# The scaled bias of the update as one GpSimd product, and the layer-1 bias of seven chunks in ten written by ScalarE

## The chip, the cores and the metric

The kernel runs on one core of a Trainium2 chip. The metric is device time in microseconds for one execution. A core has a matrix engine (TensorE, in the profile PE, with its weight loads shown apart as PEld), VectorE (DVE), ScalarE (ACT), GpSimd (POOL) and a queue engine SyncE (SP) that issues DMA transfers. The engines run side by side, each in the order of its own instructions, and wait for one another through semaphores. TensorE writes its results to PSUM banks; ScalarE and VectorE read them from there.

## The reference

A graph layer over 128 graphs of 64 nodes with 128 channels. Per edge (i, j) of the adjacency an MLP of three linear layers runs over the pair of node features; the messages of a node are summed, and a second MLP of the same form updates the node.

```python
def _mlp(x, w0, b0, g0, be0, w1, b1, g1, be1, w2, b2):
    h = jax.nn.relu(x @ w0 + b0)
    h = _layernorm(h, g0, be0)
    h = jax.nn.relu(h @ w1 + b1)
    h = _layernorm(h, g1, be1)
    return h @ w2 + b2

pair_feats = jnp.concatenate([f_i, f_j], axis=-1)
messages = _mlp(pair_feats, msg_w0, ...)
messages = messages * coupling_matrix[..., None]
agg = jnp.sum(messages, axis=2)
upd_in = jnp.concatenate([part_feats, agg], axis=-1)
updated = part_feats + _mlp(upd_in, upd_w0, ...)
```

`x` is 128 x 64 x 128 in f32; the coupling matrix is a sparse 0/1 matrix with self edges, about one entry in eight.

## The kernel before

**Tiling.** Two graphs make a pair (64 pairs); a graph has room for 640 edges. Four graphs make a quad with 20 tiles of 128 edges, and four tiles make a *chunk*: 160 chunks in all. Four pairs make a *block*, so a block is ten chunks and there are 16 blocks. Only real edges are computed; a dense path for graphs with more edges than fit stands at the end of the program and isn't entered here.

**The deferred norm.** The normalisation of layer 0 is not applied to the hidden values. The layer-1 weights are centred beforehand (`w1c`), so the product needs only a division by the standard deviation; as ReLU and the next norm don't mind a positive factor, the kernel multiplies the *bias* by the standard deviation instead. A tile's layer-1 result in bank `z` is therefore the product h x `w1c` plus the bias row `b1b` times each edge's standard deviation. That scaled bias comes into `z` in one of two ways. Either TensorE writes it first, by one matmul over 512 columns from a table (`b1t` and the turned standard deviations `sdT`, line 602); or ScalarE writes it into the bank beforehand, by four activations of 128 x 128 with the standard deviation as their scale (`seed`, line 593), and TensorE adds the products to it. Of ten chunks six are seeded, and the four others use line 602. The update's MLP has the same need once per block: `usdb` is the bias row `bu1b` scaled for each of the block's 512 nodes, made by four activations on ScalarE (`upd_shift`, line 773), and added by VectorE in `layer_out` (`uy`, line 238).

**The order of work.** It is written out by hand. A plan maps (step, place) to functions; a loop over steps runs, in each step n, the places "a" and "m" first (copies, small sums), then layer 1 of chunk n - 8, then "b", layer 0 of chunk n, the turning of chunk n - 1 with its statistics, "k" (marks and comparisons for a later pair), the statistics of chunk n - 8, and then the places "x" to "e". Every engine gets its instructions in that order and keeps to it. One step is therefore one chunk in each of two stages.

In a step, TensorE does: L605 (layer 1, into one of two `z` banks in turn), L535 (layer 0, into the only `hps` bank), L544 (turning h, into the only `hT` bank), L509 (marks); in some steps also L691 (sums over edges, 20 products of a pair at a time), L449/L451 (rows of a new half block), L736 and L750 (update), and L568, which turns the standard deviations of a quad (`sh`). ScalarE empties `z` into `y` (L608) and `hps` into `h` (L538), seeds (L593), and makes square roots: `m_sd` (L255) for a quad, `um_sd` (same line) for a block's update. VectorE makes statistics (L548 of layer 0, L615 of layer 1), `tp` (L484, an f16 comparison over 640 edges), `j` (L517) and more. GpSimd makes the variances from the statistics (L245 to L249, tiles `m` and `um`), the low parts `sh` (L563), the weights `w` (L678), the cast `i` of `tp` (L493), and the residual `xo` (L730).

**The step of `seed` and `upd_shift`.** The seed of chunk n is issued in step n + 6, two before its layer 1. Chunks whose number modulo 10 is 0, 1, 2, 6, 7, 9 are seeded. `upd_root0` of a block (which makes `um_sd`) and the first `usdb` copy stand in a step that is 9 modulo 10, the second copy one step later, the last two in the step after that, which is 1 modulo 10; `usdb` is read in step 2 modulo 10. In the step 9 modulo 10 stands also `residual` (`xo`). All this holds for the first 13 blocks, which follow `STEADY`; the last three have tables of their own (`LAST`).

Of the kernel before, what the change touches and what calls it, by code (L numbers as in the profile page):

```python
# [14 lines left out]
ALU = mybir.AluOpType  # L15
# [8 lines left out]
def tile_gnn(  # L24
# [40 lines left out]
    nc = tc.nc  # L65
    B, N, C = x.shape
    P = 128
# [9 lines left out]
    PB = 4  # L77
    NB = NP // PB
    CPB = NCHK // NB
# [88 lines left out]
    W = {}  # L168
# [62 lines left out]
    def bc(t, n, axis=1):  # L231

        s = [P, n, C] if axis == 1 else [P, C, n]
        return t.unsqueeze(axis).to_broadcast(s)
# [50 lines left out]
    def edge_path(es):  # L285
# [32 lines left out]
        def zbank(k):  # L318
            return ps_z[k].tile([P, CH * C], F32, name=f"z{k}")
# [4 lines left out]
        def at(n, place, fn, *args):  # L324
            plan.setdefault((n, place), []).append((fn, args))
# [382 lines left out]
        def wide(name, u):  # L708

            if name not in u.blk:  # L710
                u.blk[name] = updp.tile([P, PB, C], F32, name=name,
                                        bufs=2 if name in ("uo", "xo", "m0") else 1)
            return u.blk[name][:, u.q, :]
# [29 lines left out]
        def layer(u, *pairs):  # L743
            ps = u.bank()
            for q in range(u.n):
                s = slice(q * P, (q + 1) * P)
                for n, (src, w) in enumerate(pairs):
                    l = (u.blk["xnT"][:, (u.k0 + q) * P:(u.k0 + q + 1) * P] if src == "xn" else
                         getattr(u, src)[:, s])
                    nc.tensor.matmul(ps[:, s], lhsT=l, rhs=w, start=(n == 0),  # L750
                                     stop=(n == len(pairs) - 1))
            u.l_ps = ps[:, 0:u.n * P].rearrange("p (q c) -> p q c", q=u.n)
# [16 lines left out]
        def upd_shift(u, q0, q1):  # L769
            if q0 == 0:  # L770
                u.usdb = wide("usdb", u)
            for q in range(q0, q1):
                nc.scalar.activation(u.usdb[:, q, :], W["bu1b"], AF.Copy, scale=u.sd[:, q:q + 1])

# [54 lines left out]
        for b in reversed(range(NB)):  # L829
            o = b * CPB  # L830
            n = o + QC + SC

            if b < NB - 1:
                t = STEADY if b < NB - 3 else LAST[b - NB + 3]
                units = [(Unit(b, 0, PB, nc.gpsimd, ubank), n, t, 0, t[5] - 1)]
                if b == NB - 2:
                    units = [units[0][:3] + (-5, -4)]
            else:
                units = [(Unit(b, 2, 2, nc.vector, lambda: zbank(1), tbank), NCHK + L1 + 1, LAST[3], 1, 1),
                         (Unit(b, 0, 2, nc.gpsimd, lambda: zbank(0), hbank), NCHK + L1 - 1, LAST[2], 3, 3)]  # L840
            for u, n, t, m0_at, xo_at in units:
                at(n + m0_at, "m", bias0, u)
                at(n + xo_at, "e", residual, u)
                at(n + t[0], "a", sums_out, u)
                at(n + t[1], "x", turn, u, "ysum")
                at(n + t[2], "a", turn_out, u, "ysum")
                at(n + t[3], "x", lambda u: layer(u, ("xn", u0a), ("ysumT", W["w2u"])), u)
                at(n + t[4], "m", layer_out, u, "uh", "m0")
                at(n + t[4], "e", upd_m0, u)
                at(n + t[5], "x", turn, u, "uh")  # L850
                at(n + t[6], "a", turn_out, u, "uh")
                at(n + t[7], "a", upd_root0, u)
                if t is STEADY:
                    for k, q0, q1 in ((0, 0, 1), (1, 1, 2), (2, 2, PB)):
                        at(n + t[7] + k, "x", upd_shift, u, q0, q1)
                else:
                    at(n + t[7], "x", upd_shift, u, 0, u.n)
                at(n + t[8], "x", lambda u: layer(u, ("uhT", W["u1c"])), u)
                at(n + t[9], "m", layer_out, u, "uy", "usdb")
                at(n + t[9], "e", upd_m1, u)  # L860
                at(n + t[10], "x", turn, u, "uy")
                at(n + t[11], "a", turn_out, u, "uy")
                at(n + t[12], "a", upd_root1, u)
                at(n + t[12], "m", upd_inverse, u)
                at(n + t[13], "x", lambda u: layer(u, ("uyT", W["u2c"])), u)
                at(n + t[14], "m", finish, u)
        for p in range(NP):
            n = p * TG * 2 // CH
# [18 lines left out]
        for q in range(NQ):  # L887
            n = q * QC + QC if q else LEAD
# [10 lines left out]


        for n in range(2, NCHK - L1):
            if n % CPB in (0, 1, 2, 6, 7, 9):
                at(n + L1 - 2, "x", seed, n)


# [153 lines left out]
    with ExitStack() as es:  # L1059
        es.enter_context(tc.manual_schedule())  # L1060
        flag = edge_path(es)
# [160 lines left out]
```

## Time and profile before

| What | Value |
|---|---|
| Median of 9 runs | 575.0 us (573.81 to 577.68) |
| The profiled execution | 575.01 us |
| Its span, first to last instruction | 573.2 us |
| Granted TensorE clock | 0.989 of full speed |
| Bias matmuls L602 | 70, median 478 ns |
| Seeds L593 | 360 activations, median 371 ns |
| Copies L773 | 64 activations, median 392 ns |
| DMA | 63.23 MB moved, mean 110 GB/s |

The profile is one execution on the chip. A timeline row reads: start and duration in us, engine, line, operation, the tiles written and read, their shapes, the number of instructions merged into the row, and in brackets how long the engine was idle before it and what ended that wait. A matmul's duration includes the time that it spends in the array beside its neighbours, so its cost is read from the distance of starts. Tile names in the profile are cut: `um_sd` is the standard deviation of the update's block, `m_sd` that of a quad, `m_d` and `m_s` are intermediate sums, and `um` and `m` the variances' sums. Rows with the same line, such as L255, differ by tile.

### The profile page before, as it was taken

The numbers are of one execution on the slowest core, as the hardware profiler recorded it, in microseconds if no ns is written. First come the engines' busy times: TensorE is split into PE (matmuls) and PEld (weight loads), VectorE is DVE, ScalarE is ACT, GpSimd is POOL, SyncE is SP. The second block draws the span as 40 slices with busy tenths as digits, with TensorE's granted clock in tenths as the row PEclk, the third lists the DMA queues.
The fourth block names the chain that finished last, engine by engine and source line by source line (L and its number), as shares of the span: only waits on it lengthen the run. The fifth ranks groups of instructions, "written<-read, shape, count | busy, mean of one in ns | idle before, by whom it ended". The sixth has DMA issues, their size and how long they took to land. (4 is left out here: it accounts for less than half of the span.)

```text
span 573.2 us, 15824 instructions
## 1 busy us (share of the span) xinstructions
PE 551.8 (96%) x5339; PEld 518.5 (90%) x5339; DVE 479.5 (84%) x1944; ACT 476.3 (83%) x1149; POOL 339.6 (59%) x898
## 2 busy tenths in 40 slices
PE   8799899999999999999999999999999999989894
PEld 7587889999999999999999999999999999979883
DVE  6758788997979899797989889798989979786686
ACT  7678979898988889898988999898888989875434
POOL 3625466665657676565757666565767656545342
PEclk9889999999999999999999999999999999998999
DMA  4554646455654645644555545447454545432101
GB/s 102 124 134 110 129 113 136 91 132 112 107 149 110 132 102 143 113 112 126 125 139 107 138 106 132 107 109 153 113 137 87 127 115 108 113 93 28 39 19 42
DMA packets 90770, 63.23 MB, mean 110 GB/s; under 512 B 57398, under 2 KB 74812, under 8 KB 90684
## 3 DMA queue, kind: packets, MB, share of 16 engines
q1 hardware_dynamic: 90396, 62.03, 48.7%
q8 instruction: 44, 0.72, 0.6%
q14 instruction: 42, 0.34, 0.2%
q10 hardware_dynamic: 288, 0.13, 0.1%
HBM read 6.82 MB, written 4.19 MB: 19 GB/s over the span
## 5 line engine op out<-in xcount | busy, mean ns | idle before, releaser
L548 DVE BATCH_NORM_STATS2 st<-hT 128x6 f32<-128x128 f32 x640 | 142.0, 284 | 37.8 <-PE hT L544 36.2
L605 PE MATMUL z<-w1c,h 128*128 128x128 f32 x1280 | 172.5, 278 | 0.0
L605 PEld LDWEIGHTS z<-w1c,h 128*128 128x128 f32 x1280 | 161.5, 192 | 8.0 <-issue 5.1
L593 ACT ACTIVATE z<-b1b,m_sd 128x128 f32<-128x128 f32 x360 | 133.5, 371 | 8.7
L615 DVE BATCH_NORM_STATS2 st<-y 128x6 f32<-128x128 f32 x640 | 137.6, 277 | 2.7 <-ACT y L608 1.4
L608 ACT ACTIVATE y<-z 128x512 f32<-128x512 f32 x160 | 94.5, 591 | 26.5 <-PE z L605 24.8
L538 ACT ACTIVATE h<-hps,b0c 128x512 f32<-128x512 f32 x160 | 109.4, 684 | 2.2 <-PE hps L535 2.2
L544 PE MATMUL hT<-ident,h 128*128 128x128 f32 x640 | 97.9, 276 | 1.8 <-DVE st L548 1.6
L678 POOL TENSOR_TENSOR w<-oh,m_q 128x320 f32<-128x320 f16 x126 | 91.9, 741 | 9.9 <-PE hT L544 5.3
L535 PE MATMUL hps<-s,abl 128*128 128x512 f32 (+3 forms) x256 | 92.1, 371 | 2.0 <-ACT h L538 1.5
L544 PEld LDWEIGHTS hT<-ident,h 128*128 128x128 f32 x640 | 76.5, 141 | 12.7 <-DVE st L548 1.9
L493 POOL CAST i<-tp 128x640 fp32r<-128x640 f16 x58 | 41.6, 718 | 70.0 <-DVE tp L484 49.1
L535 PE MATMUL hps<-s,abh 128*128 128x512 f32 (+3 forms) x256 | 78.9, 327 | 0.0
L691 PE MATMUL ys<-y,w 128*64 128x128 f32 x1280 | 76.9, 275 | 0.0
L691 PEld LDWEIGHTS ys<-y,w 128*64 128x64 f32 x1280 | 69.2, 137 | 4.2 <-issue 3.6
L245 POOL TENSOR_TENSOR m_d<-st 128x20 f32<-128x20 f32 x62 | 16.3, 263 | 88.5 <-DVE st L548 76.7
L517 DVE TENSOR_TENSOR j<-mk,cmpt 128x320 fp32r<-128x320 f32 x124 | 58.7, 474 | 1.5 <-PE mk L509 1.5
L478 ACT ACTIVATE d<-slot,mid 128x640 f16<-128x640 f16 x64 | 52.7, 823 | 0.0
L535 PEld LDWEIGHTS hps<-s,abl 128*128 128x128 f32 x256 | 49.4, 193 | 3.3 <-ACT h L538 2.3
L535 PEld LDWEIGHTS hps<-s,abh 128*128 128x128 f32 x256 | 49.5, 193 | 0.0
L469 DVE TENSOR_TENSOR abl<-mu,abh 128x512 fp32r<-128x512 f32 (+1 forms) x33 | 22.3, 675 | 30.9 <-ACT abh L463 30.7
L463 ACT CAST abh<-mu 128x512 fp32r<-128x512 f32 (+1 forms) x33 | 18.9, 571 | 23.8 <-PE mu L451 23.8
(226 smaller groups left out, 1007.4 us busy)
## 6 DMA issues: line engine op xcount, KB each, us to landing
s<-i SPq DMA_DIRECT2D x124, 160.0 KB, 2.6
s<-j SPq DMA_DIRECT2D x124, 160.0 KB, 2.6
xn<-in_x_dram SPq DMA_DIRECT2D x15, 256.0 KB, 3.7
out_dram<-uo SPq DMA_DIRECT2D x15, 256.0 KB, 2.4
an<-in_adj_dram SPq DMA_DIRECT2D x16, 128.0 KB, 2.6
oh<-tp SPq DMA_TRANSPOSE x64, 3.4
xn<-in_x_dram SPq DMA_DIRECT2D x2, 128.0 KB
out_dram<-uo SPq DMA_DIRECT2D x2, 128.0 KB, 2.6
```

The costliest lines, as they stand in the source:

```text
L478: nc.scalar.activation(D[p], slot, AF.Abs, bias=blocks[b]["mid"][:, q:q + 1], scale=-1.0)
L517: nc.vector.tensor_tensor(JR[p][:, c], MK.pop((p, k))[:, 0:HC], cmpt[:, c], op=ALU.is_equal)
L535: nc.tensor.matmul(ps[:, c:c + w], lhsT=ab[:, g % 4, :], rhs=s, start=(k == 0), stop=(k == 1))
L538: nc.scalar.activation(H[n], ps, AF.Relu, bias=b0c)
L544: nc.tensor.transpose(ps[:, t, :], H[n][:, t * P:(t + 1) * P], ident)
L548: nc.vector.bn_stats(ST0[q][:, CH * c + t, :], ps[:, t, :])
L593: nc.scalar.activation(Z[n][:, t, :], W["b1b"], AF.Copy, scale=SR[q][:, k:k + 1])
L605: nc.tensor.matmul(ps[:, t, :], lhsT=h[:, t * P:(t + 1) * P], rhs=W["w1c"], start=False, stop=True, skip_group_check=True)
L608: nc.scalar.activation(Y[n], ps, AF.Relu)
L615: nc.vector.bn_stats(ST1[q][:, CH * c + t, :], Y[n][:, t, :])
L678: (nc.vector if p == NP - 2 else nc.gpsimd).tensor_tensor(WT[p][:, :, g, :], OH[p][:, :, g * N:(g + 1) * N], Q[q][:, k:k + TG].unsqueeze(2 ...
L691: nc.tensor.matmul(YS[b][g * N:(g + 1) * N, k, :], lhsT=w[:, t, g, :], rhs=y, start=(t == 0), stop=(t == TG - 1))
```

## The change

Three edits. `upd_shift` gets a branch: where it is called for all four rows of a block it issues one GpSimd product of 128 x 4 x 128, the bias row broadcast over the four node tiles times the standard deviation broadcast along the channels, in place of four ScalarE copies. For the 13 blocks that follow `STEADY` it is called so once, in place "e" of the step in which `um_sd` is made, instead of in three pieces in three steps; it thereby comes on GpSimd directly after `xo` and before the cast `i` of the next step. For the other blocks the four (or two) ScalarE copies are issued by two calls (or one) of two rows, at the same step. And the condition for seeding takes in the chunks that are 5 modulo 10 and over 10, where a seed by ScalarE replaces line 602.

```diff
         def upd_shift(u, q0, q1):
             if q0 == 0:
                 u.usdb = wide("usdb", u)
+            if q1 - q0 == PB:
+                nc.gpsimd.tensor_tensor(u.usdb, bc(W["bu1b"], PB),
+                                        u.sd.unsqueeze(2).to_broadcast([P, PB, C]), op=ALU.mult)
+                return
             for q in range(q0, q1):
                 nc.scalar.activation(u.usdb[:, q, :], W["bu1b"], AF.Copy, scale=u.sd[:, q:q + 1])
...
                 if t is STEADY:
-                    for k, q0, q1 in ((0, 0, 1), (1, 1, 2), (2, 2, PB)):
-                        at(n + t[7] + k, "x", upd_shift, u, q0, q1)
+                    at(n + t[7], "e", upd_shift, u, 0, PB)
                 else:
-                    at(n + t[7], "x", upd_shift, u, 0, u.n)
+                    for q0 in range(0, u.n, 2):
+                        at(n + t[7], "x", upd_shift, u, q0, q0 + 2)
...
         for n in range(2, NCHK - L1):
-            if n % CPB in (0, 1, 2, 6, 7, 9):
+            if n % CPB in (0, 1, 2, 6, 7, 9) or (n > CPB and n % CPB == 5):
                 at(n + L1 - 2, "x", seed, n)
```

In the code P and C are 128, PB is 4 (node tiles of a block), CPB is 10 (chunks of a block), NCHK is 160 and L1 is 8.

## The prediction

> **What bounds the kernel now.** I read the page's busy list first, then busy time by windows over three blocks, then the timeline of single stretches.
>
> ```profile
> PE 551.8 (96%) x5339; PEld 518.5 (90%) x5339; DVE 479.5 (84%) x1944; ACT 476.3 (83%) x1149; POOL 339.6 (59%) x898
> ...
> 366.61:399.46 32.85, 32.85 (x331) 31.39 (x330) 28.94 (x120) 29.32 (x72) 21.21 (x56) 1.00 0.56 122
> 399.46:432.31 32.85, 32.85 (x332) 31.40 (x330) 28.95 (x120) 29.32 (x72) 21.20 (x56) 1.00 0.54 121
> 432.31:465.16 32.85, 32.85 (x331) 31.39 (x330) 28.96 (x120) 29.33 (x72) 21.22 (x56) 1.00 0.51 118
> ```
>
> After the span the window rows give busy PE, PEld, DVE, ACT and POOL. A block (ten chunks) takes 32.85 us, the same three times over, and PE has no gap in it. DVE idles 3.9 us, ACT 3.5, POOL 11.6. A busy PE need not be a full one, but the starts of its matmuls follow each other at constant distances (0.112 us from one L605 to the next), so it is PE's own throughput that sets the block. What leaves PE is gained; what delays PE is lost. The page's chain of waits names only the last store's DVE op and is of no use.
>
> **What leaves PE.** Two stretches, one with the bias matmul L602, one without:
>
> ```profile
> 306.33 0.30 PE L509 MATMUL mk<-tp,posall 128*128 128x320 f16 x1
> 306.36 0.50 PE L602 MATMUL z<-b1t,sdT 80*128 80x512 f32 x1
> 306.70 0.38 PE L605 MATMUL z<-w1c,h 128*128 128x128 f32 x2
> ...
> 303.14 0.30 PE L509 MATMUL mk<-tp,posall 128*128 128x320 f16 x1
> 303.28 1.05 PE L750 MATMUL mu<-u1c,uhT 128*128 128x128 f32 x8
> ```
>
> From the L509 start to the next 128-column matmul it is 0.37 us with L602 between and 0.14 without: 0.23 us (0.233 in ns), not the 0.48 that the row states as L602's duration. The Trainium skill, "TensorE: Matmul & The Clock Gate", section "Back-to-back issue gap", gives columns / 2.4 + 2.5 ns for an isolated warm matmul: 216 ns at 512 columns; the trace's 233 is near it and is what I use. The new condition adds chunks 15, 25, ... 145, 14 in all: 14 x 0.233 = 3.26 us. The 306.36 instance is one of them (chunk 85).
>
> **ScalarE.** Off: four L773 per block for 13 blocks; two stand at 304.14 with 0.68 us together, so 0.29 apart, 1.17 a block. On: four L593 in 14 chunks, 1.51 us from the first to what follows (306.68 to 308.19). Net +0.34 us a block against 3.5 us idle. (The rewritten loop for the last blocks issues the same copies at the same place: nothing.) By place: the seed of chunk 85 comes in the step where two L773 stood (304.14), so that step grows by 0.92 us:
>
> ```profile
> 304.14 0.68 ACT L773 ACTIVATE usdb<-bu1b,um_sd 128x128 f32<-128x128 f32 x2
> 304.73 0.25 ACT L573 CAST sdT<-ma 80x128 fp32r<-80x128 f32 x1
> 305.61 0.60 ACT L608 ACTIVATE y<-z 128x512 f32<-128x512 f32 x1 [0.63 <-PE z L605]
> ```
>
> 0.63 of it fills the wait shown. The y after it starts about 0.2 to 0.3 us late, and so does the next h (306.10 to 306.78). PE's next L535 needs that h evacuated, since hps has one bank; it starts at 307.51, or 307.28 after the saving, so of 0.73 us some 0.2 remain. The following y and h are later still, but PE then spends 3 us on L691 and L449, and ACT catches up before L463 at 312.12 (it idled 0.59 there). The seed itself ends near 305.9; its L605 is at about 306.5. Cost: nothing, with 0.2 us of cover; every tenth beyond is paid 14 times.
>
> **GpSimd.** One 128x512 product a block. Its price: pos (L384), like it f32 with one operand broadcast along the row, takes 506 ns at 192 columns and 612 at 256, 1.66 ns a column, so 1.035 us at 512; b1t (L655), 80x512 with both operands broadcast as here, has a median of 1.034. Above stands xo (L730), 128x512 but with rows read in full: 1.274. The skill, "GPSIMD Engine Reference", section "3.1 Elementwise — side-by-side cycle accounting", has 2.6 cycles an element for two inputs, an estimate of 1.11 us plus dispatch, between the two. I take 1.035; the ends are 0.95 and 1.274.
>
> POOL has room: behind the new product in its queue are only the cast L493 and then L245, which waited 2.36 us for DVE. The j and oh transfers on SP sit behind the cast's stack copy; the cast moves 0.6 us, and its rows are read five chunks later. But the product's place decides:
>
> ```profile
> 330.33 0.31 ACT L255 ACTIVATE um_sd<-um,eps_c 128x4 f32<-128x4 f32 x1
> 330.92 0.38 DVE L484 TENSOR_SCALAR tp<-d,deg 128x640 f16<-128x640 f16 x1
> 331.37 0.72 POOL L493 CAST i<-tp 128x640 fp32r<-128x640 f16 x1 [3.52 <-DVE tp L484]
> 331.68 0.89 DVE L548 BATCH_NORM_STATS2 st<-hT 128x6 f32<-128x128 f32 x4 [0.38 <-PE hT L544]
> 332.84 0.60 PE L544 MATMUL hT<-ident,h 128*128 128x128 f32 x4
> ```
>
> It waits for um_sd (end 330.64) and, with the 0.078 us that POOL takes after ACT in the sh pair, starts at 330.72: 0.2 us before DVE's tp. The skill, "SBUF — State Buffer", section "Who interferes with whom", says that a 2-port DVE op and a GpSimd op exclude each other for the whole instruction, and "VectorE: DVE Perf Modes", section "What auto-detection actually checks", lets a 16-bit one-source SBUF op such as tp take such a mode. The trace agrees:
>
> ```profile
> 26.29 1.42 POOL L655 TENSOR_TENSOR b1t<-b1mix,tile_of 80x512 fp32r<-80x512 f32 x1
> ...
> 26.80 1.09 DVE L484 TENSOR_SCALAR tp<-d,deg 128x640 f16<-128x640 f16 x1
> ```
>
> tp took 1.09 instead of 0.37 and ended 0.18 us after the product. So here: the product ends at 331.75, tp at 331.93, the next DVE op can start 0.08 before that end, 331.85 in place of 331.68: DVE is 0.17 us late. First in line is hT at 332.84, which needs this L548 (end 332.57): 0.27 less 0.17 leaves 0.10, above the 0.056 us that PE needs after DVE in the shortest cases. Second is a chain that runs with DVE from there: L548, POOL's five sums for m, ACT m_sd, ACT sh, POOL sh, then the turn L568. sh ends at 304.00 and L568 starts 0.170 later. Where L568 really waited (75.28) it started 0.055 after sh and took 0.308 against 0.273; so slack is 0.170 - 0.055 - 0.035 = 0.08. DVE's 0.174 (in ns) exceeds it: PE loses 0.093 us. In 12 of the 13 blocks (in the last, at 494.6, tp comes 0.445 after um_sd and L548 1.20 after, too late to matter): 12 x 0.093 = 1.12 us.
>
> After L568 the tightest DVE return is hT at 308.11, with L548 done at 307.77: 0.34 less (0.233 - 0.093) leaves 0.20. DVE had idled 0.44 before 303.41 and is back in step there.
>
> **Sum.** -3.26 + 1.12 = -2.1 us on the profiled execution's 575.01 (span 573.2), which is the median of the runs shown, 575.0. Forecast 572.9. The first of the 14 chunks falls at 77 us, where PE still waited for other engines; it may bring up to 0.2 less.
>
> **Rivals.** *No loss to the lock* (the product ends by 331.65, or tp isn't held): the full 3.26, 571.8. For it: 0.95 us would do. Against: two rows agree on 1.03, and the held tp is in the trace. *A slow product:* at xo's 1.274 DVE is 0.41 late, PE loses 0.41 - 0.08 = 0.33 a block, 12 x 0.33 = 4.0, net +0.7: 575.7, slower than before. One mechanism, the lock at 330.72; it decides from 1.21 us on (0.27 + 0.08 = 0.35 late), and from about 1.36 us the loss passes 0.3%. For it: same bytes as xo. Against: xo's second operand isn't constant along the row. *ScalarE becomes the bound* in the step with the new seed: if h is 0.15 later than I have it, beyond the cover, 14 x 0.15 = 2.1 us go back: 575.0. For it: ACT is 89% busy in a block; against: the 3 us of L691 and L449 right behind. That the change doesn't do what it says is excluded by the order of instructions: 14 fewer L602, 13 L773 on POOL behind xo.
>
> **Numbers.** Chances: forecast 0.50, no loss 0.20, slow product 0.15, ScalarE 0.10, others 0.05. About 0.3% (1.7 us) is what a measurement can tell from no change. The forecast's own spread, 572.3 to 573.6, lies for three quarters under 573.3; with the no-loss case faster comes to 0.57; slow product and ScalarE fall mostly inside the 0.3%, same 0.31; slower 0.12, should the product be longer or both losses meet. Range 571.5 to 575.8, from just under the no-loss case to the slow product.
>
> **What would show it.** A POOL row L773, 13 times, near 1.03 us; tp's largest steady duration near 1.0 us, once a block; L602 56 times; blocks near 32.71 us; L568 waiting for POOL sh about 0.1 us a block. A block of 32.6 means no loss; over 32.85, the slow product, with DVE waits ahead of hT; waits of L535 for ACT h mean ScalarE. I am wrong if another place loses: tp unharmed but PE waiting on POOL's or ACT's other products.

## The result, and the profile after

The changed kernel takes 572.4 us (median of 10 runs, 570.5 to 573.3) against 574.9 (median of 31). The ratio is 0.9945, with a 95% interval of 0.993 to 0.9961: 2.2 to 4.0 us less, which is more than the noise of the measurement. Below, *before* and *after* name the two kernels. The profiled execution has a span of 570.7 us. Busy time first, then three blocks by windows (the columns are those shown before: span, then PE, PEld, DVE, ACT and POOL with their numbers of instructions, the granted clock, the DMA share and GB/s), then the product's row among the instructions that touch `usdb`:

```profile
PE 549.1 (96%) x5325; PEld 515.0 (90%) x5325; DVE 483.2 (85%) x1944; ACT 480.7 (84%) x1153; POOL 352.5 (62%) x911
```

```profile
265.27:297.90 32.63, 32.63 (x330) 31.13 (x329) 29.19 (x118) 29.59 (x72) 22.20 (x57) 1.00 0.52 124
297.90:330.53 32.63, 32.63 (x330) 31.13 (x329) 29.19 (x118) 29.59 (x73) 22.20 (x57) 1.00 0.56 123
330.53:363.17 32.64, 32.64 (x329) 31.12 (x329) 29.20 (x118) 29.58 (x73) 22.21 (x57) 1.00 0.52 114
```

```profile
L773 POOL TENSOR_TENSOR usdb<-bu1b,um_sd x13: 1039/1039/1041, 102.6 to 493.9; 128x512 f32<-128x512 f32 x13
```

PE has 14 instructions less, and the same block took 32.85 us before: 0.22 us less in each. POOL's 13 products have the priced duration. DVE is *busier* by 0.25 us a block, though its work is the same: the comparison `tp` takes 0.64 us longer beside the product, and other rows are a little shorter. The timeline of that place (start and duration in us; in brackets the idle time before, with what ended it; here and below, rows of other instructions are left out):

```profile
298.05 0.31 ACT L255 ACTIVATE um_sd<-um,eps_c 128x4 f32<-128x4 f32 x1
298.44 1.04 POOL L773 TENSOR_TENSOR usdb<-bu1b,um_sd 128x512 f32<-128x512 f32 x1 [2.87 <-ACT um_sd L255]
298.65 1.02 DVE L484 TENSOR_SCALAR tp<-d,deg 128x640 f16<-128x640 f16 x1
299.58 0.88 DVE L548 BATCH_NORM_STATS2 st<-hT 128x6 f32<-128x128 f32 x4
300.51 0.42 PEld L544 LDWEIGHTS hT<-ident,h 128*128 128x128 f32 x4 [0.23 <-DVE st L548]
300.56 0.61 PE L544 MATMUL hT<-ident,h 128*128 128x128 f32 x4
...
301.15 0.25 DVE L274 RECIPROCAL m_q<-m_sq 128x20 f32<-128x20 f32 x1
301.33 0.81 DVE L548 BATCH_NORM_STATS2 st<-hT 128x6 f32<-128x128 f32 x4
...
304.37 0.27 POOL L563 TENSOR_TENSOR sh<-m_sd,sh 128x40 fp32r<-128x40 f32 x1
...
304.75 0.27 PE L568 MATMUL ma<-ident,sh 128*80 128x128 f32 x1
```

The second L548 of the stretch as it was in the kernel before, with the `hT` matmuls that the first one waited for:

```profile
331.04 0.60 PE L544 MATMUL hT<-ident,h 128*128 128x128 f32 x4
...
333.26 0.26 DVE L274 RECIPROCAL m_q<-m_sq 128x20 f32<-128x20 f32 x1
333.47 0.89 DVE L548 BATCH_NORM_STATS2 st<-hT 128x6 f32<-128x128 f32 x4
```

and the end of the chain that runs from there, in another block of the kernel before:

```profile
303.73 0.27 POOL L563 TENSOR_TENSOR sh<-m_sd,sh 128x40 fp32r<-128x40 f32 x1
...
304.17 0.27 PE L568 MATMUL ma<-ident,sh 128*80 128x128 f32 x1
```

Three readings, counted from the end of `um_sd` (330.64 before, 298.36 after). The first L548 starts 1.04 us later before and 1.22 after: DVE is 0.18 late. The second L548 ends 3.72 later before and 3.78 after: only 0.06 late. And `sh` ends 0.17 us ahead of L568 before (304.00 to 304.17) and 0.11 after (304.64 to 304.75), still twice the 0.055 at which PE really waits. Between the two L548 about 0.12 us were won back: DVE follows the L274 sooner (0.18 us after its start, not 0.21) and takes 0.81 us for four tiles, not 0.89. In the kernel before, the second L548 was waiting for `hT` too, though the row shows no idle time: it starts 0.03 to 0.04 us after the last of the four `hT` matmuls ends (332.84 + 0.60 to 333.47), just as the first L548 does, which shows the wait (331.04 + 0.60 to 331.68). In after it starts 0.16 us behind them (300.56 + 0.61 to 301.33): that wait is gone. Why the four tiles then also take 0.08 us less is not shown.

**Where the time went.** Set side by side chunk by chunk, by the start of the first L605, the two profiled executions give: 14 steps of about -0.24 us, at chunks 15, 25 and so on to 145, which is -3.4; about +0.02 us a block elsewhere, +0.3 in sum; and two differences that have nothing to do with the change, +2.10 us before chunk 0 and -1.61 between chunks 148 and 149. Both of these are stretches with half the TensorE clock, and the second profile of the changed kernel, further down, has them otherwise. The first two rows are of the kernel before, the last of the kernel after; the third figure from the right is the clock:

```profile
24.84:31.70 6.86, 5.76 (x23) 4.40 (x21) 3.65 (x9) 4.81 (x13) 5.72 (x6) 0.50 0.25 59
516.40:519.80 3.40, 3.40 (x18) 3.30 (x17) 0.17 (x1) 2.15 (x7) 1.03 (x3) 0.50 0.00 0
```

```profile
25.64:35.90 10.26, 8.98 (x36) 7.67 (x35) 5.26 (x14) 5.93 (x15) 5.44 (x5) 0.50 0.44 116
```

So the spans' difference of 2.5 us looks like the forecast's 2.1, but the steady part is -3.1: the agreement of two single spans was partly luck. From here on kernels are compared by their steady block (the distance from one block's first L435 to the next) and by the ratio of their timed runs, never by two spans.

### The profile page after: what moved, and what is told of

The parts are those of the page before. It is cut to its first block, busy times and chain, and to the rows that moved or that the text cites. A ratio compares the mean times of both kernels' runs of the same rounds, so it can differ in the third digit from the quotient of the medians.

```text
span 570.7 us, 15800 instructions
## 1 busy us (share of the span) xinstructions
PE 549.1 (96%) x5325; PEld 515.0 (90%) x5325; DVE 483.2 (85%) x1944; ACT 480.7 (84%) x1153; POOL 352.5 (62%) x911
## 5 line engine op out<-in xcount | busy, mean ns | idle before, releaser
L605 PE MATMUL z<-w1c,h 128*128 128x128 f32 x1280 | 172.0, 277 | 0.0
L548 DVE BATCH_NORM_STATS2 st<-hT 128x6 f32<-128x128 f32 x640 | 140.9, 282 | 32.3 <-PE hT L544 31.6
L605 PEld LDWEIGHTS z<-w1c,h 128*128 128x128 f32 x1280 | 160.3, 192 | 7.6 <-issue 4.3
L593 ACT ACTIVATE z<-b1b,m_sd 128x128 f32<-128x128 f32 x416 | 154.3, 371 | 10.1
L544 PE MATMUL hT<-ident,h 128*128 128x128 f32 x640 | 98.0, 276 | 1.8 <-DVE st L548 1.6
L535 PE MATMUL hps<-s,abl 128*128 128x512 f32 (+3 forms) x256 | 92.1, 371 | 2.1 <-ACT h L538 1.7
L544 PEld LDWEIGHTS hT<-ident,h 128*128 128x128 f32 x640 | 75.4, 141 | 13.8 <-DVE st L548 4.6
L535 PE MATMUL hps<-s,abh 128*128 128x512 f32 (+3 forms) x256 | 78.6, 325 | 0.0
L535 PEld LDWEIGHTS hps<-s,abl 128*128 128x128 f32 x256 | 49.3, 193 | 3.5 <-ACT h L538 2.5
L535 PEld LDWEIGHTS hps<-s,abh 128*128 128x128 f32 x256 | 49.5, 193 | 0.0
L509 PE MATMUL mk<-tp,posall 128*128 128x320 f16 x126 | 38.0, 302 | 0.0
```

Of the source, the lines that this page charges most:

```text
L535: nc.tensor.matmul(ps[:, c:c + w], lhsT=ab[:, g % 4, :], rhs=s, start=(k == 0), stop=(k == 1))
L544: nc.tensor.transpose(ps[:, t, :], H[n][:, t * P:(t + 1) * P], ident)
L548: nc.vector.bn_stats(ST0[q][:, CH * c + t, :], ps[:, t, :])
L593: nc.scalar.activation(Z[n][:, t, :], W["b1b"], AF.Copy, scale=SR[q][:, k:k + 1])
L605: nc.tensor.matmul(ps[:, t, :], lhsT=h[:, t * P:(t + 1) * P], rhs=W["w1c"], start=False, stop=True, skip_group_check=True)
```

## The experiments

My theory: PE is the bound and gets about 0.235 us a block; the copies had to leave ScalarE for that; the product's hold on `tp` is absorbed. Rivals: the hold costs PE something that the block hides (the prediction's 0.093 us at L568); a longer product turns the change into a loss; the gain comes from one of the two halves alone. Each ratio is to runs of the kernel before that were taken alongside (their medians lie between 574.1 and 575.3 us), so medians of different rows aren't compared directly.

| Kernel | Median us | Ratio to before (95%) | Steady block us |
|---|---|---|---|
| before | 575 | 1 | 32.85 |
| after | 572.41 | 0.9945 (0.993 to 0.9961) | 32.63 |
| after, a second time | 571.95 | 0.9954 (0.9931 to 0.9978) | 32.63 |
| seeds alone | 575.06 | 0.9994 (0.9978 to 1.0011) | 32.98 |
| product alone | 574.28 | 0.9989 (0.9977 to 1.0001) | 32.86 |
| product behind the cast | 570.9 | 0.9935 (0.9914 to 0.9956) | 32.64 |
| product from `xn` rows | 572.15 | 0.9955 (0.9936 to 0.9973) | 32.64 |
| product of 640 columns | 574.38 | 0.9987 (0.9971 to 1.0003) | 32.85 |
| product of 768 columns | 575.24 | 1.0022 (0.9999 to 1.0046) | 33.07 |
| product of 1024 columns | 582.41 | 1.014 (1.0101 to 1.0178) | 33.50 |
| seeds at 8 in place of 5 | 588.81 | 1.025 (1.0213 to 1.0286) | 33.90 |
| seeds at 4 as well | 572.05 | 0.9947 (0.9929 to 0.9966) | 32.76 |
| seeds at 3 as well | 585.27 | 1.0185 (1.0161 to 1.0208) | 33.60 |

### Each half alone

Seeds alone: the kernel before with the new condition, the copies left on ScalarE where they were.

```diff
-            if n % CPB in (0, 1, 2, 6, 7, 9):
+            if n % CPB in (0, 1, 2, 6, 7, 9) or (n > CPB and n % CPB == 5):
```

> The kernel before with the new seeds of chunks 5 modulo 10 alone; the update's copies stay on ScalarE. Theory (the copies had to leave ScalarE to make room): ScalarE's step with the new seed then also holds two copies, 2 x 0.29 = 0.59 us more than in the changed kernel, where h was done 0.24 us ahead of L535 (0.06 of that is needed), so PE waits about 0.4 us a block for h and gives back more than the 0.235 it saves: blocks of about 33.0 us, time about 577, 0.4% above before. Rival (ScalarE has room anyway, the move to GpSimd was not needed): blocks of 32.62 us, time as the changed kernel, 3.2 us below before.

Measured: blocks of 32.98 as expected, and no gain in time (575.06 us; the loss of 2 us that I expected in the timed runs doesn't show). The timeline behind the new seed shows who took the saving:

```profile
305.65 1.56 ACT L593 ACTIVATE z<-b1b,m_sd 128x128 f32<-128x128 f32 x4
...
307.79 0.68 ACT L538 ACTIVATE h<-hps,b0c 128x512 f32<-128x512 f32 x1
...
308.52 0.19 PEld L535 LDWEIGHTS hps<-s,abl 128*128 128x128 f32 x1 [0.27 <-ACT h L538]
308.52 0.44 PE L535 MATMUL hps<-s,abl 128*128 128x384 f32 x1
```

`h` ends at 308.47 and the next layer 0 starts 0.05 later, the least distance there is. Against the kernel before, PE has gained 0.23 us at the missing L602 and lost 0.35 again at this L535. In after the same `h` ends 0.24 us ahead (306.93 + 0.68 to 307.85):

```profile
306.93 0.68 ACT L538 ACTIVATE h<-hps,b0c 128x512 f32<-128x512 f32 x1
...
307.85 0.42 PE L535 MATMUL hps<-s,abl 128*128 128x384 f32 x1
```

The cover is 0.19, and it exists because the two copies left this step.

Product alone, that is the changed kernel with the old condition:

```diff
-            if n % CPB in (0, 1, 2, 6, 7, 9) or (n > CPB and n % CPB == 5):
+            if n % CPB in (0, 1, 2, 6, 7, 9):
```

> The changed kernel without the new seeds: the GpSimd product alone. Theory now (VectorE's 0.18 us are caught up before the chain to L568): blocks as before, 32.85 us within 0.02, time equal to before. The prediction's own step (0.09 us lost at L568 in 12 blocks): blocks of 32.94 us, 1.1 us slower than before. Rival (relief of ScalarE by 1.17 us a block is what gained): blocks clearly under 32.8 us.

Measured: `tp` is held to 1.015 us here as well, and the block is 32.86: the product by itself costs PE about 0.01 us a block and gains nothing. Neither half is worth anything alone; the product buys the room on ScalarE that the seeds need.

### The same product where it holds nobody

```diff
-                    at(n + t[7], "e", upd_shift, u, 0, PB)
+                    at(n + t[7] + 1, "b", upd_shift, u, 0, PB)
```

> The changed kernel with the GpSimd product issued one step later, behind the cast i, where it no longer meets tp. Theory now (the lock delays VectorE but PE does not lose by it): tp back to 0.38 us, L568 starts 0.17 us after sh again instead of 0.11, blocks stay at 32.62 us within 0.02, time equal to the changed kernel. Rival (the lock costs PE its 0.09 us in some other place): blocks of about 32.54 us, 1 us faster than the changed kernel.

```profile
229.62 0.31 ACT L255 ACTIVATE um_sd<-um,eps_c 128x4 f32<-128x4 f32 x1
230.21 0.38 DVE L484 TENSOR_SCALAR tp<-d,deg 128x640 f16<-128x640 f16 x1
230.66 0.72 POOL L493 CAST i<-tp 128x640 fp32r<-128x640 f16 x1 [3.52 <-DVE tp L484]
231.34 1.04 POOL L773 TENSOR_TENSOR usdb<-bu1b,um_sd 128x512 f32<-128x512 f32 x1
```

The timeline shows `tp` back at 0.38 us with the product behind the cast, DVE isn't late at either L548, and `sh` ends 0.17 us ahead of L568 again. The block is 32.64, as long as in after, so the hold of 0.64 us on `tp` costs PE nothing that can be read. By the prediction's own term it would have been 0.09 us a block better. Its ratio, 0.9935, and the two of after have intervals that overlap widely; the blocks decide. The second run of after:

> The changed kernel once more, for a second profile and for comparison on the same chip. Theory: blocks of 32.63 us again, 14 steps of 0.235 us; the times of half clock at the start and near 516 us may lie elsewhere and move the span by 2 us without any change of the program. Rival (they belong to the change): they are where they were in the first profile.

It has blocks of 32.63 again, and again a `tp` of 1.015 us; its half clock fell elsewhere. Layer 1 of chunk 0 begins at 33.49 us, where the first profile of the same kernel had 36.45, and from chunk 148 to 149 it takes 5.42 us, where the first had 3.80: both differences belong to the execution and not to the change. Timed runs with the same granted clock give about the block's gain: at 0.989 the median is 572.2 us (4 runs) against 575.4 for before (17), at 0.994 to 0.995 it is 570.8 (4) against 573.7 (9).

### Longer products

First try: the product reads the rows of `xn` instead of the broadcast deviation.

```diff
-                nc.gpsimd.tensor_tensor(u.usdb, bc(W["bu1b"], PB),
-                                        u.sd.unsqueeze(2).to_broadcast([P, PB, C]), op=ALU.mult)
+                nc.gpsimd.tensor_tensor(u.usdb, bc(W["bu1b"], PB), u.blk["xn"], op=ALU.mult)
```

> The changed kernel with the GpSimd product's second operand read in full rows (the block's node features stand in for the broadcast standard deviation, so the update's layer-1 bias is another number): the form of xo. Theory: the product takes 1.27 us, tp is held 0.24 us longer, VectorE is 0.42 us late; 0.12 of that it catches up and 0.08 is slack at L568, so PE loses about 0.22 us a block: blocks of 32.84 us, time about 574.4, 2.6 us above the changed kernel. The prediction's step (no catching up): 0.33 us, blocks of 32.95 us. Rival (the product's length doesn't matter to PE): 32.63 us.

This one did not test what it was made for. The product took 1.275 us, as `xo` does, but without `um_sd` among its operands it no longer waited for that; it started right behind `xo` and never met `tp` (0.38 us). It is a second placement without the hold, and its block of 32.64 says the same as the one above. The expected 32.84 was not tested by it.

Second try: the product keeps its operands and gets twice the columns, by laying `usdb` and `ysum` (not in use then) into one tile. The lines that make this tile are left out.

```diff
...
+                two = [P, 2, PB, C]
                 nc.gpsimd.tensor_tensor(
-                    u.usdb, bc(W["bu1b"], PB),
-                    u.sd.unsqueeze(2).to_broadcast([P, PB, C]), op=ALU.mult)
+                    u.blk["both"], bc(W["bu1b"], PB).unsqueeze(1).to_broadcast(two),
+                    u.sd.unsqueeze(2).to_broadcast([P, PB, C]).unsqueeze(1).to_broadcast(two),
+                    op=ALU.mult)
```

> The changed kernel with the GpSimd product twice as long (its second half goes into the tile of ysum, which is not in use then; the output is unchanged). Theory: 1.88 us at 1.64 ns a column, tp held until 0.18 us after it, VectorE about 1.02 us late; beyond the 0.2 us that are absorbed PE loses it one for one, 0.8 us a block: blocks of 33.45 us, time about 582, 10 us above the changed kernel. Rival (VectorE gets the shared port before the product ends, or PE has more slack): blocks under 33.0 us.

Measured: 1.89 us for the product, 1.87 for `tp`, blocks of 33.50. To find the point from which it starts to cost, a tile of the same kind with 640 and with 768 columns:

```diff
...
+                long = [P, PB, 5, 32]      # 768 columns: [P, PB, 3, 64]
                 nc.gpsimd.tensor_tensor(
-                    u.usdb, bc(W["bu1b"], PB),
-                    u.sd.unsqueeze(2).to_broadcast([P, PB, C]), op=ALU.mult)
+                    u.blk["both"].rearrange("p q k c -> p q (k c)")[:, :, 0:160]
+                    .rearrange("p q (k c) -> p q k c", k=5),
+                    bc(W["bu1b"], PB)[:, :, 0:32].unsqueeze(2).to_broadcast(long),
+                    u.sd.unsqueeze(2).to_broadcast([P, PB, 32]).unsqueeze(2).to_broadcast(long),
+                    op=ALU.mult)
```

> The slow product of the prediction's rival, still dependent on um_sd: the GpSimd product is made 640 columns instead of 512 (five times the first 32 columns of the bias over the rows of one tile that holds usdb and ysum), about 1.25 us; so the bias values of the update are others in this kernel. In after, VectorE is 0.18 us late behind tp and PE lost about 0.01 a block. Absorption theory (VectorE wins back about 0.12 us at the second L548, because it waited there for hT anyway, and L568 has 0.06 to 0.08 more): product 1.25, tp about 1.23, L548 0.39 late, PE loses 0.39 - 0.18 = about 0.2 a block, blocks near 32.83 us. Prediction's sum (0.08 of cover alone): PE loses 0.31, blocks near 32.95. Lock without price: 32.63.

> As the 640-column product, with 768 columns (three times the first 64 columns of the bias), about 1.46 us; the bias values of the update are others in this kernel too. Absorption theory: VectorE 0.60 late, PE loses 0.60 - 0.18 = about 0.42 a block, blocks near 33.05 us. Prediction's sum (0.08 of cover): 33.16. The difference to the 640-column kernel should be the difference of the two products, about 0.21 us a block, in both theories.

| Columns | Product us | over after's 1.039 | Block us | over after's 32.63 |
|---|---|---|---|---|
| 640 | 1.256 | 0.217 | 32.85 | 0.22 |
| 768 | 1.469 | 0.430 | 33.07 | 0.43 |
| 1024 | 1.89 | 0.85 | 33.50 | 0.87 |

From after's length on, a longer product is paid one for one. Where PE pays is in the timelines, 640 columns first, then 768:

```profile
233.99 1.26 POOL L783 TENSOR_TENSOR usdb<-bu1b,um_sd 128x640 f32<-128x640 f32 x1 [2.88 <-ACT um_sd L255]
...
234.20 1.23 DVE L484 TENSOR_SCALAR tp<-d,deg 128x640 f16<-128x640 f16 x1
...
235.35 0.88 DVE L548 BATCH_NORM_STATS2 st<-hT 128x6 f32<-128x128 f32 x4
...
236.28 0.42 PEld L544 LDWEIGHTS hT<-ident,h 128*128 128x128 f32 x4 [0.44 <-DVE st L548]
236.28 0.66 PE L544 MATMUL hT<-ident,h 128*128 128x128 f32 x4
```

```profile
234.02 0.42 PEld L544 LDWEIGHTS hT<-ident,h 128*128 128x128 f32 x4 [0.66 <-DVE st L548]
234.02 0.66 PE L544 MATMUL hT<-ident,h 128*128 128x128 f32 x4 [0.22 <-DVE st L548]
```

It is the turning L544, which needs the `hT` bank that L548 empties, and not L568. In after the load of its weights already waits (0.23 us on DVE), but it starts 0.05 us ahead of its matmul and so beside the matmul before: next to nothing is lost. The second `hT` matmul follows the first by 0.12 us instead of 0.11, which is about the 0.01 us a block that the product alone costs. With 640 columns load and matmul start together. Against after, the first `hT` matmul comes 0.17 us late and the second 0.21, and the lateness stays at that to the end of the block. `sh` still ends 0.11 us ahead of L568, and with 768 and 1024 columns 0.10 to 0.12, so L568 waits in none of the kernels with a longer product. My expectation for 640 columns gave the right size, 0.2 us, by the wrong place ("L568 has 0.06 to 0.08 more"): what DVE wins back at the second L548 doesn't help a PE that was stopped one step earlier.

DVE's lateness with 640 columns is 0.18 + 0.22 = 0.40 us, PE's 0.21. So this place takes 0.19 us of lateness, and after uses 0.18: the kernel stands on the edge, and this is why the hold is free at 512 columns and costs at 640.

### More seeds

If ScalarE's room counted by average (it idles 3.0 us a block in after), chunks other than 5 should do as well.

```diff
-            if n % CPB in (0, 1, 2, 6, 7, 9) or (n > CPB and n % CPB == 5):
+            if n % CPB in (0, 1, 2, 6, 7, 9) or (n > CPB and n % CPB == 8):
```

> The changed kernel with chunks 8 modulo 10 seeded instead of 5: the same share, the same L602 removed, another place. Theory (ScalarE's room is one of place, not of its average): the 1.51 us come in a step where h is done 0.70 us ahead of L535 and no long work of PE follows, so PE waits about 0.9 us a block: blocks of 33.5 us, time about 582. Rival (only the sum of ScalarE's work counts): blocks of 32.63 us, time equal to the changed kernel.

For the other two the last number is replaced: `n % CPB in (4, 5)` and `n % CPB in (3, 5)`.

> After, with the chunks 4 modulo 10 seeded too (8 of 10). ScalarE gets 1.5 us more a block, in the step from which one copy was taken (0.29 us). If room by average counts (ACT idles 3.0 us a block in after), 15 more steps of -0.235 us: blocks near 32.40, 568.5 us. If room is of place (as with chunks 8): h comes too late for the next L535 with a slack at the minimum of 0.05, and the saving is given back or more: blocks 32.7 to 33.5.

> After, with the chunks 3 modulo 10 seeded too (8 of 10), whose seed falls in the step of um_sd, from which one copy was taken. By average: blocks near 32.40, 568.5 us. By place: um_sd itself comes later, the product with it, and h waits: blocks 32.7 to 33.5.

None gives the block that the average promises (32.63 with 8 in place of 5, 32.40 for eight chunks in ten), and two lose more than I expected: 33.90 for 33.5 with 8, 33.60 for at most 33.5 with 3. The waits, in the kernel with 8 for 5 and in the one with 3 and 5:

```profile
256.64 0.19 PEld L535 LDWEIGHTS hps<-s,abl 128*128 128x128 f32 x1 [0.63 <-ACT h L538]
256.64 0.33 PE L535 MATMUL hps<-s,abl 128*128 128x128 f32 x1 [0.44 <-ACT h L538]
```

```profile
239.56 0.28 DVE L274 RECIPROCAL m_q<-m_sq 128x20 f32<-128x20 f32 x1 [0.90 <-ACT m_sq L269]
...
240.63 0.33 PE L535 MATMUL hps<-s,abl 128*128 128x128 f32 x1 [0.57 <-ACT h L538]
...
242.14 0.31 ACT L255 ACTIVATE m_sd<-m,eps_c 128x20 f32<-128x20 f32 x1 [0.59 <-POOL m L249]
...
243.12 0.31 PE L568 MATMUL ma<-ident,sh 128*80 128x128 f32 x1 [0.18 <-POOL sh L563]
```

In both, `h` comes too late for L535, and more of ScalarE's results are late with it. With 8 for 5 the weights of L736 also wait 0.37 us for ScalarE's copy `ysumT` (L741), and those of L568 0.28 us for `sh`. With 3 and 5, `m_sq` is late, the L274 on VectorE waits 0.90 us for it, and the L548 behind that, GpSimd's `m` and then `m_sd` and `sh` follow late. With chunks 4 the loss is smaller:

```profile
237.25 0.31 ACT L255 ACTIVATE m_sd<-m,eps_c 128x20 f32<-128x20 f32 x1
237.59 0.22 ACT L562 CAST sh<-m_sd 128x40 fp32r<-128x40 f32 x1
237.89 0.27 POOL L563 TENSOR_TENSOR sh<-m_sd,sh 128x40 fp32r<-128x40 f32 x1 [0.29 <-ACT sh L562]
238.21 0.12 PEld L568 LDWEIGHTS ma<-ident,sh 128*80 128x80 f32 x1 [0.26 <-POOL sh L563]
```

Here `sh` comes 0.30 us later than in after, by the seed that now stands ahead of `m_sd` on ScalarE (in after `m_sd` had waited 0.21 us for GpSimd's `m`; here ScalarE has no idle time before it). PE is 0.24 us late at L568, which is all that the missing L602 behind it saves, and about 0.1 us more at the next L535: 0.13 us a block worse than after. Its timed runs (0.9947) don't separate from after's; that it isn't better is read from the blocks. No kernel here beats after by more than its interval.

## Why the prediction came out right, and the term in it that was wrong

The direction and the size were right, 572.9 forecast and 572.4 measured, but one term of the sum was wrong, and the two medians lie so close partly by luck. By its steps:

- **PE as the bound, L602 at 0.233 us.** Right: 0.24 between the two profiles, 0.233 with the seeds alone. All 14 chunks show it, chunk 15 too, for which the prediction had allowed up to 0.2 us less.
- **ScalarE for nothing, with 0.2 us of cover at L535.** Right: 0.24 us of slack, of which 0.05 is needed. The seeds alone show what stands behind this: without the copies' leaving, the same step loses 0.35.
- **The product at 1.035 us.** Right: 1.039. It follows the row with the same broadcast (`b1t`) and not the one with the same bytes (`xo`); the product that read full rows took 1.275.
- **Start 0.08 us behind `um_sd`, `tp` held to about 1.0 us, DVE 0.174 us late.** Right: 0.078, 1.015 and 0.18. The Trainium skill, "SBUF — State Buffer", section "Who interferes with whom", has a 2-port VectorE instruction and a GpSimd instruction exclude each other for the whole instruction, and the trace agrees at four lengths: `tp` takes 1.02, 1.23, 1.44 and 1.87 us beside products of 1.04, 1.26, 1.47 and 1.89, and ends 0.18 us after each of them.
- **hT keeps 0.10 us against 0.056 needed.** Right to the hundredth, 300.46 to 300.56. This, and not L568, was the margin that decides.
- **L568 loses 0.093 us in 12 blocks, +1.12 us.** Wrong; this is the term that failed. L568 loses nothing: from the end of `um_sd` to its start it is 6.38 to 6.39 us before and 6.39 after, and `sh` ends 0.11 us ahead of it against 0.055 needed. All places together lose 0.01 us a block (the product alone) to 0.02 (the two profiles), at most 0.3 in sum. The prediction carried DVE's 0.174 us along the chain undiminished. But the second L548 on that chain had been waiting for PE's `hT`, and an engine that waits there wins back lateness: 0.06 arrived, less than the slack of 0.08. Of the 0.12 won back about 0.04 is that wait, and the rest is the shorter L548, whose reason stays open. The 0.035 us that the prediction set aside for an L568 that does wait is borne out: in the kernel with 3 and 5, L568 waits, and the L605 behind it starts 0.38 us after it, against 0.34 in after.

So the sum is -3.4 + 0.3 = -3.1 us, nearer to the value of the rival *no loss to the lock*, 571.8, than to the forecast. The rival's reasons (a shorter product, or a `tp` that isn't held) were both wrong: the lock is there in full, and its delay is absorbed. The ratio, 2.2 to 4.0 us of gain, holds 3.1 and just misses 2.1; the blocks tell the two apart by themselves (32.63 measured, 32.71 expected).

*A slow product* was tested and is nearly what the prediction said, in another place. It put the point from which the change turns into a loss at a product of 1.21 us, by L568; the 1.256 us product leaves the block at before's length, through `hT`. At the 1.274 us that it named, the loss would be 0.235 a block by the one-for-one rule, 12 x 0.235 = 2.8 us, where the prediction had 4.0: next to no change, not +0.7 us. The prediction was right to keep the product's duration as the number on which the sign hangs. *ScalarE as the bound* didn't happen here, but it does as soon as chunks 3, 4 or 8 are seeded or the copies stay.

## What to carry to other kernels

When work moves from the busiest engine to another, what counts is the other's room at that *place*: give its average idle time no weight, and find the next instruction of the bound that waits for it. When you carry a delay along a chain, stop at every step where the late engine used to wait anyway and take that wait off; and look at the first consumer with little slack before the last, since a bound that was stopped early can't be stopped again for the same delay. Here `tp` ended 0.18 us after the product that held it, at all four lengths, so the length of such a product should be compared with the slack behind it before its place in the queue is chosen.

## What the hardware showed that was not expected

- The half clock on PE comes in stretches of about 3.4 us or multiples (3.4, 6.8 and 10.2 us here): once from about 25 us on, once from a point between 511 and 528 us on, and again at the end of every profile. The first two are not in every execution of the same kernel: after had 10.2 us of it near the start in one profile, and in the other none there and 3.4 us at 512. PE waits near both places, 1.41 us (L180) and 1.91 us (L736), but it waits as long in the executions that keep the full clock there. The start alone differs by 2.96 us between the two profiles of after, more than the effect that was forecast. What sets it off was not tried.
- PE counts as busy while it is late. With 640 columns the window over a block has PE busy 32.83 of 32.84 us, though each block is 0.22 us longer than in after: a matmul that waits for its weights is merely longer (0.66 us for four in place of 0.61). Only the distance of starts shows the loss.
- The product's length is linear in its columns: (1.89 - 1.039) / 512 = 1.66 ns a column, with about 0.19 us on top; with full rows as second operand 512 columns take 1.275.
